# Keeping both halves of one batch's second FFN out of attention, in place of one

## The chip, the cores and the metric

The kernel runs on one core of a Trainium2 chip. The metric is the device time of one execution in microseconds (us). The kernel before has a median of 2063.42 us over 3 runs (2063.11 to 2066.16). All times below are microseconds unless they are marked ns.

A core has five engines that run side by side, each through its own list of instructions in a fixed order: TensorE (PE, matmuls; its weight loads are PEld), VectorE (DVE), ScalarE (ACT), GpSimd (POOL) and SyncE (SP), which here only issues DMA transfers. They wait for one another by semaphores. Matmul results land in PSUM, everything else lives in SBUF.

## The reference

The input is 4 batches of 1024 tokens with 256 features. Each batch goes through three residual blocks:

```
x = x + 0.5 * ffn(layernorm(x))     # first FFN
x = x + attn(layernorm(x))
x = x + 0.5 * ffn(layernorm(x))     # second FFN, the same weights

ffn(x):  scores = sigmoid(x @ gate_W) * route_scale          # 8 experts, the best 2 count
         h = gelu(x @ W1[e] + b1[e]);  y = h @ W2[e] + b2[e]   # for every expert, 256 -> 128 -> 256
         out = sum_e gate[e] * y[e] + shared expert
attn(x): h = softmax(q k / 16 + mask) v @ Wo + bo + x        # 16 heads of 64, 1024 x 1024 scores a head
         out = gelu_tanh(layernorm(h) @ W1 + b1) @ W2 + b2 + h  # an MLP, 256 -> 512 -> 256
```

The reference computes all eight experts for every token and weights them with the gates, and the kernel does the same, so an FFN is dense work: nine experts (the shared one is number 8), each with two small matmuls.

## The kernel before, in words

**Tiling.** Tokens lie on partitions in tiles of 128. An FFN is done for half a batch (512 tokens) at a time, as a *job* (class `Job`, made by `ffn`, line 1086 on): `prep` (layer norm statistics, normalisation L919, turning the tokens so that features lie on partitions, the router), then for each of the nine experts a hidden *layer* (6 matmuls of 512 columns, gelu, times the gate, split into a high and a low 16-bit part), then four *seconds* (one for each tile of 128 tokens, 27 matmuls of 256 columns and one for the bias). Every product is done as three 16-bit matmuls on high and low parts (`mm3`, L970). The attention block's MLP is a job as well (`mlp`), with four layers and four seconds.

**Attention.** A step is one head, half the queries and 256 of the keys. Its loop (`attention`) runs 512 steps. A step's instructions are: maxima of a later step's scores (two matmuls, L1467, and a reduction on DVE, L1474), the scores (four matmuls of 512 columns, L1531 and L1532, into the one PSUM slot S1), the exponential on ScalarE (L570, `pt`), its high part on ScalarE (L1543, `pk`), its low part on GpSimd (L1546), and 24 short matmuls with the values (L1581 to L1584, into `av`). Every fourth step also turns a row of maxima (L1501) and puts it in place (L1505, one DMA).

**Filler.** TensorE's time between these steps is given to other work: projections of later heads (`wq`), output projections of earlier ones (`wo`), and the FFN and MLP jobs (rank 3, generator `serve`). The class `Order` is a planner that runs when the kernel is built: it keeps an estimated clock for every engine, and at each point of the attention loop it picks what TensorE does next by ranks, costs and due times (`pick`, `RATE`, `NEAR`, `LEAD`). What it picks is the order that every engine's list then has; inside attention nothing reorders it.

**Two forms of an FFN.** In attention (`burst` false) the input is turned by DMA (L924, L926, L927), the gates are stored to DRAM (L1068) and come back as eight broadcasts of 256 KB (L1120), and the low part of a hidden piece is made on GpSimd (L1186). In the other form (`burst` true; `spread` in the code) the input is turned by TensorE (L939, evicted at L941 and L943), the gates are spread by a matmul with a selector (L1165), and the low part is made on DVE (L1194).

**The end.** Batch 3 is last. Its own MLPs and second FFNs cannot start before its attention has ended, so they form a tail, done by `run_jobs`: the next job's layers are mixed with the seconds of the one before, and its `prep` is drawn in between. Hidden pieces of neighbouring jobs lie by turns in `hp` and in tiles that attention has left (`pt`, `pk`), inputs by turns in `xF` and `aT`. In this part the order is set by the framework's own scheduler from the program's order.

**KEEP.** The jobs of batch nb-2 = 2 that come after its attention are two MLP halves and two FFN halves, in this order. `queue` puts the last `KEEP` of them on the list `kept`; `serve` does not start a kept job, and `back` gives kept FFN halves the `burst` form. A kept half therefore runs first in the tail. Its `prep` may still be drawn into attention, but `prepare` does so only for the job at the head of the list.

```
            self.kept = jobs[-KEEP:]                                              # queue
        kept = range(2 - KEEP, 2) if b == self.nb - 2 else ()                     # back
                ... and self.jobs[0].prepared and self.jobs[0] not in self.kept   # serve
```

Of the kernel before, what the change touches and what calls it, by code (L numbers as in the profile page):

```python
# [36 lines left out]
CW2 = 32.0  # L37
NOSYNC = mybir.DependencyInfo(mybir.DependencyClass.NoSync, mybir.DependencyReason.DATA)
ORDER = (8, 0, 1, 2, 3, 4, 5, 6, 7)
KEEP = 1  # L40
SPL = 1
OD = 3
TQ = 0
# [264 lines left out]
class Kernel:  # L308
# [1468 lines left out]
    def queue(self, jobs, b=None):  # L1777

        if b == self.nb - 2:
            self.kept = jobs[-KEEP:]  # L1780
        if b == 0:
# [4 lines left out]
    def back(self, b):  # L1786
# [9 lines left out]
        def half_h(half):  # L1796
            return lambda: h[:, half * 4:half * 4 + 4]

        def after(half):
            getattr(nc, QO).dma_start(self.half_of(self.a["out"][b], half), half_h(half)())  # L1800
            yield 0

        m = [self.mlp(b, half, half_h(half)(), burst) for half in range(2)]
        kept = range(2 - KEEP, 2) if b == self.nb - 2 else ()
        self.last = [self.ffn(half_h(half), 2 * b + 1, half, burst or half in kept, lambda half=half: after(half), m[half])
# [122 lines left out]
```

## Time and profile before

| | |
|---|---|
| median of 3 runs | 2063.42 |
| profiled execution, time | 2060.11 |
| its span | 2058.2 |
| mean granted TensorE clock | 0.994 |
| busy: PE / ACT / POOL / DVE | 95% / 73% / 73% / 69% |
| instructions | 53009 |

The profile's page gives each engine's busy time, and the span in 40 slices of 51.5 us with the busy share in tenths. Matmuls overlap in the records: one of 512 columns is shown as 0.38 long, while the next may start 0.215 behind it. So a busy TensorE is not a full one, and the working below counts from start to start. The granted clock is 1.00 or 0.50 in pieces; a stretch's value is their mean. Chains and waits name what ended an idle time last.

Parts of the last 250 us, as they lie in the trace: batch 2's first FFN half has its layers at 1840.5 to 1852.2 in one block, and its seconds spread over the steps up to 1899; the last score step starts at 1912.15; the kept half's layers run from 1926.37 to 1938.45; then come the two MLP halves and the two FFN halves of batch 3, the last matmul at 2053.6.

### The profile page before, as it was taken

To read this page: it belongs to the slowest core of one execution; us is meant where nothing else is said; L and a number is where in the kernel's file an instruction comes from. 1 tells how busy PE (TensorE), PEld (TensorE's weight loads), DVE (VectorE), ACT (ScalarE), POOL (GpSimd) and SP (SyncE) were. 2 spreads that over 40 slices of the span, in tenths; PEclk is the share of its full clock that TensorE was granted. 3 is DMA by queue.
4 is the path that set the end of the run, shared out by engine and by line. 5 is a ranking of instruction groups with operands and counts; after the bars stand their busy time and mean duration, and the time that the engine had idled before them with its cause. 6 is when DMAs were issued, how large, how long until landed. Compare 5 with 4: busy or idle time off the path is not lost. (4 is left out here: it accounts for less than half of the span.)

```text
span 2058.2 us, 53009 instructions
## 1 busy us (share of the span) xinstructions
PE 1960.8 (95%) x22468; PEld 1282.9 (62%) x22468; DVE 1413.6 (69%) x2372; ACT 1499.1 (73%) x1785; POOL 1498.0 (73%) x979
## 2 busy tenths in 40 slices
PE   6989999999999999999999999999999999999878
PEld 2546576766666556666666666656676666667545
DVE  6576676766767777775767667777767576866465
ACT  6437878768766787778787778687877777778563
POOL 7737787768767988778777887777776888778310
PEclk9999999999999999999999999999999999999999
DMA  6543233333513314243333333323324414251000
GB/s 175 152 128 84 75 91 96 75 87 61 143 36 86 89 32 108 49 100 93 81 81 70 98 76 85 92 70 76 81 48 104 114 40 106 48 111 36 11 21 21
DMA packets 213019, 166.21 MB, mean 81 GB/s; under 512 B 140991, under 2 KB 172872, under 8 KB 212782
## 3 DMA queue, kind: packets, MB, share of 16 engines
q1 hardware_dynamic: 212782, 162.83, 32.1%
q8 instruction: 176, 2.88, 0.6%
q14 instruction: 61, 0.50, 0.1%
HBM read 70.18 MB, written 13.83 MB: 41 GB/s over the span
## 5 line engine op out<-in xcount | busy, mean ns | idle before, releaser
L1546 POOL TENSOR_TENSOR pk<-pt,pk 128x1024 f16<-128x1024 f32 x512 | 1087.3, 2132 | 258.9 <-ACT pk L1543 173.0
L1474 DVE TENSOR_REDUCE mx<-S 128x1 f32<-128x1024 f32 x512 | 626.1, 1223 | 298.1 <-PE S L1467 273.1
L570 ACT ACTIVATE pt<-S 128x1024 f32<-128x1024 f32 x512 | 523.8, 1023 | 353.8 <-PE S L1532 334.5
L1543 ACT CAST pk<-pt 128x1024 f16<-128x1024 f32 x512 | 534.6, 1045 | 15.7 <-DMA aT<-pk 0.7
L1584 PE MATMUL av<-V,pk 128*128 128x65 f16 x4096 | 428.7, 192 | 25.7 <-POOL pk L1546 24.7
L1583 PE MATMUL av<-V,pk 128*128 128x64 f16 x4096 | 435.0, 195 | 0.0
L1581 PE MATMUL av<-V,pk 128*128 128x65 f16 x4096 | 434.0, 193 | 0.7 <-DVE at L1597 0.7
L1581 PEld LDWEIGHTS <-pk 128*128 128x128 f16 x4096 | 382.0, 96 | 54.0 <-issue 0.3
L1583 PEld LDWEIGHTS <-pk 128*128 128x128 f16 x4096 | 380.3, 97 | 52.9 <-issue 1.1
L1584 PEld LDWEIGHTS <-pk 128*128 128x128 f16 x4096 | 379.9, 99 | 30.9 <-POOL pk L1546 30.6
L1531 PE MATMUL S<-low 128*128 128x512 f16 x1024 | 388.2, 379 | 6.4 <-ACT pt L570 5.7
L1532 PE MATMUL S<-AC 128*128 128x512 f16 x1024 | 388.4, 379 | 0.0
L1467 PE MATMUL S<-AC 128*128 128x512 f16 x1024 | 304.4, 379 | 7.9 <-DVE mrow L1505 4.7
L970 PEld LDWEIGHTS <-hp 128*128 128x128 f16 x2100 | 204.6, 98 | 71.8 <-issue 6.2
L970 PE MATMUL F<-xA,wq 128*128 128x512 f16 x768 | 187.4, 381 | 0.0
L970 PE MATMUL F<-wfs,hp 128*128 128x256 f16 x1404 | 176.1, 273 | 1.7 <-POOL hp L1186 0.8
L1532 PEld LDWEIGHTS <-AC 128*128 128x128 f16 x1024 | 100.0, 98 | 115.1 <-issue 27.5
L1531 PEld LDWEIGHTS <-low 128*128 128x128 f16 x1024 | 100.0, 98 | 103.9 <-issue 0.6
L1186 POOL TENSOR_TENSOR hp<-u,hp 128x512 f16<-128x512 f32 x88 | 100.5, 1156 | 78.1 <-ACT hp L1183 71.5
L970 PEld LDWEIGHTS <-wfs 128*128 128x128 f16 x864 | 83.7, 99 | 111.3 <-issue 20.9
L970 PE MATMUL F<-xF,wfs 128*128 128x512 f16 x576 | 139.5, 388 | 7.6 <-DVE gb L642 4.2
L970 PEld LDWEIGHTS <-wq 128*128 128x128 f16 x768 | 74.8, 98 | 84.2 <-issue 1.9
(240 smaller groups left out, 2526.2 us busy)
## 6 DMA issues: line engine op xcount, KB each, us to landing
AC<-qk SPq DMA_DIRECT2D x128, 256.0 KB
gb<-gd SPq DMA_DIRECT2D x88, 256.0 KB
low<-qk SPq DMA_DIRECT2D x64, 256.0 KB
wq<-wqd SPq DMA_DIRECT2D x33, 384.0 KB
hp<-mwd SPq DMA_DIRECT2D x6, 1024.0 KB
x<-in_L_attn_x_dram SPq DMA_DIRECT2D x8, 512.0 KB
x1d<-x SPq DMA_DIRECT2D x8, 512.0 KB
wo<-wod SPq DMA_DIRECT2D x16, 256.0 KB
```

The lines of the kernel that those rows point to most:

```text
L570: i = self.nc.scalar.activation(out, in_, func, **kw).ins
L970: i = self.nc.tensor.matmul(*args, start=start, **kw).ins
L1186: nc.gpsimd.tensor_tensor(hp[e][:, 1], u, hp[e][:, 0], ALU.subtract)
L1467: mm(ps[:, hs], AC[:, 0, qs], AC[:, 1, hs], start=True, stop=(h == 0 or t > 0), skip_group_check=True)
L1474: nc.vector.tensor_reduce(self.mx[:, t % 4:t % 4 + 1], ps, AX.X, ALU.max, negate=True)
L1531: mm(o, low[:, 1, ks], low[:, 0, qs], start=True, stop=False, skip_group_check=True)
L1532: mm(o, AC[:, 1, ks], AC[:, 0, qs], start=False, stop=True, skip_group_check=True)
L1543: nc.scalar.copy(pk[:, 0], pt[:])
L1546: nc.gpsimd.tensor_tensor(pk[:, 1], pt[:], pk[:, 0], ALU.subtract)
L1581: mm(o[:, 0:65], pk[:, 0, ps], v[:, 0:65], start=(n == 0 and c == 0 and t == 0), stop=False, skip_group_check=True)
L1583: mm(o[:, 0:64], pk[:, 0, ps], v[:, 65:129], start=False, stop=False, skip_group_check=True)
L1584: mm(o[:, 0:65], pk[:, 1, ps], v[:, 0:65], start=False, stop=(n == 3 and c == 1), skip_group_check=True)
```

## The change

`KEEP` is 2 where it was 1: both halves of batch 2's second FFN are kept, take the `burst` form, and run first behind attention. All other constants, the planner's rate among them, stay.

```
 ORDER = (8, 0, 1, 2, 3, 4, 5, 6, 7)
-KEEP = 1
+KEEP = 2
 SPL = 1
```

With 2, the list's head after the MLP halves is the first FFN half, and it stays there until attention ends; so `prepare` draws the first half's preparation into attention, and the second half's is left to the tail. On TensorE the two kernels' lists agree up to the score step that starts at 1803.89.

## Prediction

> **What bounds the kernel now.** I read the page first.
>
> ```profile
> PE 1960.8 (95%) x22468; PEld 1282.9 (62%) x22468; DVE 1413.6 (69%) x2372; ACT 1499.1 (73%) x1785; POOL 1498.0 (73%) x979
> PE   6989999999999999999999999999999999999878
> POOL 7737787768767988778777887777776888778310
> ```
>
> After the start TensorE is at nine tenths or more until 1904 us and lower behind it, where GpSimd falls to nothing: attention ends there and a tail of FFN work follows. Then the table by stretch, cut at starts of matmuls (columns: stretch, its length, busy PE, PEld, DVE, ACT, POOL, clock, DMA share, GB/s).
>
> ```profile
> 1803.89:1839.67 35.78, 33.96 (x449) 23.19 (x447) 26.58 (x51) 26.78 (x30) 27.88 (x15) 1.00 0.62 127
> 1839.67:1912.15 72.48, 69.53 (x843) 47.08 (x842) 39.78 (x77) 60.39 (x73) 55.71 (x34) 1.00 0.15 42
> 1912.15:1926.37 14.22, 10.26 (x125) 7.41 (x122) 6.34 (x18) 6.44 (x9) 7.13 (x7) 0.88 0.00 1
> 1926.37:1938.45 12.08, 12.08 (x58) 5.47 (x56) 7.15 (x14) 7.18 (x12) 1.60 (x4) 1.00 0.00 0
> 1938.45:1963.93 25.48, 21.02 (x158) 15.14 (x156) 15.29 (x25) 15.11 (x28) 10.12 (x8) 1.00 0.21 62
> 2005.20:2040.38 35.18, 30.38 (x211) 19.20 (x210) 19.99 (x48) 18.39 (x31) 1.60 (x4) 0.95 0.00 1
> ```
>
> In order: stretch A, before the first FFN of batch 2 starts; B, the last 21 score steps, with that FFN between them; C, the end of attention; the hidden layers of the kept FFN alone; its second layers with batch 3's first MLP; and last the "twin", where batch 3's second FFN is laid over its first. TensorE fills A, B and the kept layers; in the twin it does not. Third, what attention does with no FFN between its steps (ScalarE's timeline):
>
> ```profile
> 1819.36 1.02 ACT L570 ACTIVATE pt<-S 128x1024 f32<-128x1024 f32 x1 [0.98 <-PE S L1532]
> 1820.41 1.04 ACT L1543 CAST pk<-pt 128x1024 f16<-128x1024 f32 x1
> 1821.55 1.02 ACT L570 ACTIVATE pt<-S 128x1024 f32<-128x1024 f32 x1
> 1822.61 1.04 ACT L1543 CAST pk<-pt 128x1024 f16<-128x1024 f32 x1
> 1823.75 1.02 ACT L570 ACTIVATE pt<-S 128x1024 f32<-128x1024 f32 x1
> ```
>
> Exponentials start 2.20 apart. One PSUM slot holds the scores: four matmuls (0.86, starts 0.215 apart), their drain, then exp (1.02), then the next four. TensorE needs only 0.73 (values) + 0.43 (maxima) + 0.86 = 2.03 of it. By the starts of L1531, 88 steps of the whole trace hold neither filler nor a row of maxima: median 2.20, mean 2.39. So filler hides 0.17 or more a step, and attention without filler is bound by the score slot and not by TensorE. Last, the chain of waits at the end of attention:
>
> ```profile
> 1919.42 0.20 POOL fnb L901
> ...
> 1919.65 2.07 ACT ld L919 x4
> 1921.73 0.48 ACT aT L1439
> ...
> 1922.22 0.70 DVE aT L1441
> ```
>
> Four normalisations for batch 3's first MLP run on ScalarE ahead of the copy that the last output projection waits for.
>
> **The change part by part.** The instruction order is the same on TensorE until the step at 1803.89. From there batch 2's first FFN leaves B for the tail; its preparation stays in A, in the TensorE form; the second FFN's preparation leaves B for the tail. The sum is against the profiled execution (2060.11, span 2058.2), which lies 3.3 below the median 2063.42; I add the difference to the median.
>
> *A (35.78 now).* Removed: two casts, two GpSimd subtractions (1.16 each) and two transposing DMAs for the input, a gate store, later eight 256 KB broadcasts on SP. SP's other transfers pass earlier; only one DVE wait of 1.9 for a broadcast shows there. Added: two groups of transposes (0.44 each) with their evictions, and four normalisations (2.07) drawn into one ScalarE block. By the new order's steps, each at the length such a step has in the trace: 2.91 (two transposes) + 3.32 + 3.49 + 2.63 (router) + 2.20 + 3.37 + 2.90 + 3.34 + 3.34 + 3.78 + 3.51 = 34.8, so 1.0 less, mostly a 1.53 stall inside the router (waiting for a transposing DMA) that goes. Behind the ScalarE block the exponentials queue, and the values behind them: up to 2.07 back. I take 0.5 less (1.1 more to 1.5 less).
>
> *B (72.48 now).* The 54 first-layer matmuls (0.216 each: 11.7) and 112 second-layer ones (0.109: 12.2) go, with two table loads and the second FFN's transposes, router and gates (1.9). Of the 21 steps, 15 are then bare, 3 carry a row of maxima (17 bare such in the trace, 2.20 to 4.89; the last 2.91), one a row without maxima, one attention's transposes and a selector matmul, one the 12 matmuls of the output projection (3.87 now). 15 x 2.20 + 3 x 2.90 + 2.2 + 2.4 + 3.87 = 50.2. One pair's GpSimd subtraction (L1414, 2.13) was under FFN matmuls; bare, GpSimd (2.09 apart when saturated) regains 0.1 a step, so it delays the values by 0 to 2.13: I take the middle, 1.1. Sum 51.3, saved 21.2. Bounds: rows at 2.20 and no delay 48.0 (saved 24.5); bare steps at the mean and rows at 3.60, 55.4 (saved 17.1). TensorE work of 25.8 leaves, so 4.6 of it does not come back: that is the cover lost.
>
> *C (14.22 now).* The four normalisations for the MLP move behind the kept FFN's hidden layers, so the copy can start at 1919.87 in place of 1921.63: 1.8 less (0 if GpSimd or the table load gates it; 3.1 if the half-clock window in this stretch, clock 0.88, goes with the stall).
>
> *Tail.* One FFN more: layers 11.7, second layers 12.2, eight selector matmuls 1.7, router 0.6, transposes 0.9, gates 0.4: 27.5 of TensorE if all is covered, the lower bound. The first kept FFN's 12.08 of layers stand as they do now; what is inserted is the stretch from their end to the end of the second one's layers. Its order is the twin's: few second-layer matmuls, transposes, router, three layer matmuls, router, fifteen, then the rest mixed. The twin takes 35.18 for the same content; 10.0 of it pass before its router starts, as the first column tile waits for the last hidden piece, and gelu waits for the router's table switch. The four normalisations (2.07) now stand ahead of that switch: upper bound 37.3. Against it the selectors come earlier: after the layers' end DVE has 9 x 0.69 = 6.2 to do for the last pieces, so the router may start some 2 sooner. These about cancel: 35.0. What follows (the MLP's layers, 1938.45 on) keeps its order but for where its layer matmuls lie: 0, give or take 1.
>
> One rule speaks against the change. The Trainium skill, "ScalarE: Activation LUTs", section "What ACT_TABLE_LOAD costs", gives each switch a 1.28 load and a 1.38 drain. In the twin the load at 2015.82 ends at 2017.11 and the router's exp starts at 2017.12: the load agrees, the drain isn't there. The two switches move from attention into the tail's chain; with drains the sum would be 2.8 longer.
>
> Sum: +35.0 - 0.5 - 21.2 - 1.8 = **+11.5**: 2071.6 for a profiled execution, **2074.9** beside the median. Ends: 27.5 - 1.5 - 24.5 - 3.1 = -1.6 and 37.3 + 1.1 - 17.1 + 0 + 1 = +22.3.
>
> **The rivals.** The measurement tells 0.2% (4.1 us) from no change.
> 1. *TensorE is the bound on both sides.* B gives back 24.5, C 1.8, and the second FFN hides its own start: 27.5 - 24.5 - 1.8 - 0.5 = +0.7, 2064. For it: PE 95%. Against it: the twin's 35.18 for 27.5 of work, and 2.20 steps. Chance 0.08.
> 2. *Faster: the extra FFN fills the tail's stalls.* TensorE stands still 4.2 before 1963.93, 1.8 before 1968.45, some 5 between 1976.9 and 1983.6. If the extra second-layer matmuls covered these 11.0 and B gave the full 24.5: 35.0 - 0.5 - 24.5 - 1.8 - 11.0 = -2.8, 2060.6. It decides once over 11.5 are covered at my B, or over 8.2 at that one. Against it: in the new order the extra FFN is done before the MLP's last layer matmuls. Chance 0.03.
> 3. *Attention without filler is slower still.* Bare steps at the mean, rows at 3.60, no gain in C, tail 37.3: 37.3 - 0.5 - 17.1 = +19.7, 2083. For it: several bare steps of 3.2 to 3.9, where GpSimd or ScalarE lag. Chance 0.14.
> 4. *The first FFN is served in attention anyway.* The order shows no layer matmul between the steps of B: 0.
>
> **How the numbers follow.** Forecast 0.75, rivals 0.08, 0.03, 0.14 and 0. Range 2066 to 2083: the lower end is rival 1 with a little lost, the upper rival 3. Slower takes the forecast, rival 3 and a little of rival 1's edge, less the forecast's low edge: 0.88; same 0.08; faster 0.04.
>
> **What would show it.** B's 21 score steps at 50 to 52, exponentials 2.2 apart; eight fewer GpSimd subtractions at L1186, eight fewer broadcasts, eight more selectors at L1165; the copy L1439 with no normalisation ahead of it; 35 between the layers of the two kept FFNs, with TensorE idle before the router. Wrong if steps in B run at 2.05, or if the new stretch in the tail runs at 28 or at 40.

## The result, and the profile after

| | before | changed |
|---|---|---|
| median | 2063.47 (4 runs, 2063.11 to 2066.16) | 2076.57 (4 runs, 2076.37 to 2077.79) |
| profiled execution, span | 2060.11, 2058.2 | 2077.79, 2076.0 |

The changed kernel is slower by 13.1: ratio 1.0067, 95% interval 1.0055 to 1.0079. The forecast was 11.5 slower.

The page of the changed kernel, the lines that answer to those shown of the kernel before:

```profile
PE 1971.0 (95%) x22484; PEld 1287.6 (62%) x22484; DVE 1420.1 (68%) x2382; ACT 1499.4 (72%) x1784; POOL 1487.0 (72%) x969
PE   6989999999999999999999999999999999998888
POOL 7637787768767987778786987877777888776100
```

TensorE's share is still 95%, so the page's first line does not show the change. GpSimd falls to nothing a slice earlier: attention ends earlier and the tail is longer. The table by stretch shows it (changed kernel; columns as in the prediction: stretch, length, busy PE, PEld, DVE, ACT, POOL, clock, DMA share, GB/s):

```profile
1806.50:1843.10 36.60, 34.79 (x456) 24.23 (x455) 28.27 (x55) 27.83 (x33) 27.95 (x17) 1.00 0.41 95
1843.10:1894.65 51.55, 46.51 (x642) 29.41 (x641) 24.59 (x32) 44.45 (x44) 45.21 (x22) 1.00 0.08 17
1894.65:1905.91 11.26, 8.39 (x123) 6.62 (x120) 5.17 (x16) 4.26 (x5) 6.24 (x7) 1.00 0.01 2
1905.91:1918.00 12.09, 12.09 (x59) 5.48 (x56) 7.49 (x17) 7.19 (x12) 1.60 (x4) 1.00 0.01 1
1918.00:1953.02 35.02, 30.98 (x216) 20.16 (x215) 19.88 (x46) 17.78 (x30) 3.23 (x3) 0.95 0.09 27
1953.02:1979.87 26.85, 20.46 (x154) 14.78 (x153) 15.72 (x26) 16.20 (x29) 6.87 (x6) 0.98 0.13 44
2022.58:2057.97 35.39, 30.55 (x212) 19.48 (x210) 19.82 (x48) 18.38 (x31) 1.60 (x4) 0.95 0.00 1
```

In order: A, B, C, the layers of the first kept FFN, the inserted stretch to the end of the second kept FFN's layers, the stretch to the end of the first MLP's layers, and the twin. B lost 21 and its TensorE is busy for 46.5 of 51.6; the inserted stretch has the twin's length and its idle time. Set beside the kernel before, with a second execution of the same changed kernel (first experiment) to tell run from change, all between starts or ends of the same matmuls:

| part | before | changed | changed again | forecast of the difference |
|---|---|---|---|---|
| up to the first changed step | 1803.89 | 1806.50 | 1805.45 | 0 |
| A | 35.78 | 36.60 | 36.61 | -0.5 |
| B | 72.48 | 51.55 | 51.58 | -21.2 |
| C | 14.22 | 11.26 | 12.16 | -1.8 |
| layers of the first kept FFN | 12.08 | 12.09 | 12.09 | 0 |
| inserted FFN | - | 35.02 | 34.62 | +35.0 |
| to the end of the first MLP's layers | 25.48 | 26.85 | 26.72 | 0, give or take 1 |
| second MLP's layers | 12.99 | 13.81 | 12.75 | 0 |
| batch 3's first FFN | 28.28 | 28.90 | 28.61 | 0 |
| twin | 35.18 | 35.39 | 35.51 | 0 |
| rest | 17.8 | 18.0 | 18.0 | 0 |

The first row is no effect of the change. In the 14 traces of this study the first score step starts at 154.5 to 158.2 and the way from there to the first changed step takes 1648.5 to 1652.3, for all kernels alike; before's trace has the smallest sum of the two. So the spans differ by 17.8 and the medians by 13.1. From the first changed step on the parts add up to +15.2 and, for the repeat, +14.3; the 1 to 2 by which this is above the medians is within what single traces of one kernel differ by here.

ScalarE's timeline in B, where nothing is left between the score steps:

```profile
1854.20 1.02 ACT L570 ACTIVATE pt<-S 128x1024 f32<-128x1024 f32 x1 [1.22 <-PE S L1532]
1855.26 1.04 ACT L1543 CAST pk<-pt 128x1024 f16<-128x1024 f32 x1
1856.40 1.02 ACT L570 ACTIVATE pt<-S 128x1024 f32<-128x1024 f32 x1
1857.45 1.05 ACT L1543 CAST pk<-pt 128x1024 f16<-128x1024 f32 x1
1858.60 1.02 ACT L570 ACTIVATE pt<-S 128x1024 f32<-128x1024 f32 x1
1859.65 1.04 ACT L1543 CAST pk<-pt 128x1024 f16<-128x1024 f32 x1
1860.87 1.02 ACT L570 ACTIVATE pt<-S 128x1024 f32<-128x1024 f32 x1 [0.17 <-PE S L1532]
```

Exponentials start 2.20 apart, as forecast, and once 2.27. Of B's 21 steps fourteen take 2.19 to 2.27 and one 2.48; three with a row of maxima take 3.32, 3.28 and 3.24; one in which GpSimd also subtracts for attention's output takes 3.17; one with transposes 2.25; the one with the output projection 2.90. The chain of waits across C:

```profile
1901.77 0.67 PE F L1436 x4
1902.46 0.59 ACT aT L1439
1903.08 0.70 DVE aT L1441
1903.83 10.02 PE F L970 x55
```

The copy L1439 follows the transposes at once; no normalisation stands ahead of it. And ScalarE in the inserted FFN:

```profile
1925.55 0.58 ACT L941 CAST aT<-S 128x512 f16<-128x512 f32 x1 [1.33 <-PE S L939]
1926.03 1.09 ACT L919 ACTIVATE ld<-h,fnb,fr 128x256 f32<-128x256 f32 x2
1927.64 0.58 ACT L941 CAST aT<-S 128x512 f16<-128x512 f32 x1 [0.53 <-PE S L939]
1928.13 1.09 ACT L919 ACTIVATE ld<-h,fnb,fr 128x256 f32<-128x256 f32 x2
1929.24 1.28 ACT L570 ACT_TABLE_LOAD   x1
1930.53 0.18 ACT L570 ACTIVATE S<-S 128x32 f32<-128x32 f32 x1
1930.73 1.28 ACT L570 ACT_TABLE_LOAD   x1
1932.03 0.66 ACT L570 ACTIVATE F<-F,b1f 128x512 f32<-128x512 f32 x1
```

The first kept FFN's layers ended at 1918.00; the second one's first gelu runs at 1932.03, behind its transposes' evictions, two pairs of the MLP's normalisations, and the router's exp between two table loads. Exp starts 0.01 and gelu 0.02 behind its load: no drain.

### The profile page after: what moved, and what is told of

Its sections match the earlier page's. It is cut to its first block, busy times and chain, and to the rows that moved or that the text cites. A ratio compares the mean times of both kernels' runs of the same rounds, so it can differ in the third digit from the quotient of the medians.

```text
span 2076.0 us, 53017 instructions
## 1 busy us (share of the span) xinstructions
PE 1971.0 (95%) x22484; PEld 1287.6 (62%) x22484; DVE 1420.1 (68%) x2382; ACT 1499.4 (72%) x1784; POOL 1487.0 (72%) x969
## 3 DMA queue, kind: packets, MB, share of 16 engines
HBM read 68.09 MB, written 13.81 MB: 39 GB/s over the span
## 4 chain that ended last, share of the span: by engine, by line
PE 81%; POOL 6%; ACT 5%; DVE 4%; issue 2%; DMA 1%; SPq 0%; POOLq 0%; ACTq 0%; DVEq 0%
PE F L970 32%; PE S L1531 10%; PE S L1467 10%; PE S L1532 9%; PE av L1584 6%; PE av L1583 5%; PE av L1581 5%; POOL pk L1546 3%; PE S L970 2%; ACT pt L570 1%; ACT pk L1543 1%; DMA gb<-gd 1%; POOL hp L1186 1%; PE S L1501 1%; ACT u L570 1%
## 5 line engine op out<-in xcount | busy, mean ns | idle before, releaser
L970 PEld LDWEIGHTS <-hp 128*128 128x128 f16 x1992 | 195.5, 99 | 85.2 <-issue 11.2
L970 PE MATMUL F<-wfs,hp 128*128 128x256 f16 x1296 | 166.0, 274 | 7.8 <-ACT hp L1183 3.8
L1186 POOL TENSOR_TENSOR hp<-u,hp 128x512 f16<-128x512 f32 x80 | 91.5, 1158 | 72.3 <-ACT hp L1183 68.7
L970 PE MATMUL F<-xF,wfs 128*128 128x512 f16 x540 | 132.0, 391 | 7.7 <-DVE gb L642 4.2
```

The lines of the kernel that those rows point to most:

```text
L970: i = self.nc.tensor.matmul(*args, start=start, **kw).ins
L1186: nc.gpsimd.tensor_tensor(hp[e][:, 1], u, hp[e][:, 0], ALU.subtract)
```

## The experiments

Medians of one group of runs stand beside the kernel before of the same group (2062.82 in the first, 2063.52, 2063.93 and 2061.89 in the others).

**1. The changed kernel again.**

> The changed kernel once more, to see which stretches of the two traces differ from run to run and which by the change. Theory (the change acts only from the step at 1803.89 of before on): the stretch ahead of it, 2.61 longer in the changed kernel's trace, comes out anywhere between 1803.9 and 1806.5; B stays at 51 to 52, C at 11 to 11.5, the inserted FFN at 35.0, each within 0.3 of the first trace. The two MLP stretches (26.85 and 42.71) move by up to 1.4 if their surplus over before is run-to-run, and stay within 0.3 if it belongs to the new order. Rival: the stretch ahead is again 2.6 longer, so something of the change lies in the early part too.

2076.19 (5 runs), ratio 1.0068 (1.0056 to 1.0080). A, B, the inserted FFN and the twin repeat within 0.4. The stretch ahead came out 1.05 shorter than the first time. Of the two MLP stretches the first keeps its surplus over before (26.72 against 25.48), so that belongs to the new order; the second does not (12.75 against 12.99). C does not repeat either: 12.16 at a clock of 0.86 against 11.26 at 1.00.

**2. What attention gives back when a job leaves it and none is added.** Batch 2's first second-FFN half is left out altogether:

```
-        return m + self.last
+        if b == self.nb - 2:
+            m[0].after = lambda: after(0)
+            return m + self.last[1:]
+        return m + self.last
```

> The kernel before, one half kept, with batch 2's first second-FFN half left out altogether: that half of batch 2 is written without its second FFN. This is what attention gives back when a job leaves it, with no job added behind. Theory of the prediction (attention without filler is bound by its score slot, 2.20 a step): B falls by 20 to 22, A and C within 1 of before or C shorter by up to 3, time 2039.5 to 2043.5, against TensorE work of 27.5 that was left out. Rival (TensorE is the bound, a job costs what its matmuls cost): 25.8 to 29.5 less, 2034 to 2037.6.

2042.53 (4 runs), ratio 0.9904 (0.9891 to 0.9916): 20.3 less, inside the theory's range and outside the rival's. Its A and B:

```profile
1807.83:1841.63 33.80, 31.84 (x429) 21.30 (x427) 25.09 (x43) 26.62 (x30) 27.12 (x17) 1.00 0.40 95
1841.63:1895.41 53.78, 48.91 (x671) 31.86 (x670) 29.45 (x51) 45.51 (x46) 46.16 (x22) 1.00 0.09 21
```

A and B together lose 20.7, split otherwise than expected (A 2.0 less, B 18.7). The 27.5 in the expectation are those of the other form of an FFN; the half that was left out turns its input by DMA and has no selectors, so 11.7 + 12.2 + 0.6 + 0.4 = 24.9 of TensorE work left the kernel by the prediction's prices, and the time fell by 20.3: 4.6 of the work did not come back as time. With this run the whole change falls into two measured halves: -20.3 for taking the job out, and 2076.19 - 2042.53 = +33.7 for putting it into the tail.

**3. Is a bare step bound by the score slot or by TensorE?** The changed kernel, with a third of the value products of the last 21 steps left out:

```
-                mm(o[:, 0:65], pk[:, 1, ps], v[:, 0:65], start=False, ...)
+                if i < 491 or n == 3 and c == 1:
+                    mm(o[:, 0:65], pk[:, 1, ps], v[:, 0:65], start=False, ...)
```

> The changed kernel, where the products of the values with the low part of the probabilities are left out in the last 21 steps (8 of 24 value matmuls a step, 0.24 of TensorE's time); GpSimd still makes the low part. Theory of the prediction (a step without filler is bound by the score slot: scores, their drain, exp): bare steps stay at 2.20, B falls by 0 to 2 (only steps with rows or projections get shorter), time 2074 to 2077. Rival (TensorE bounds the bare steps): they fall to 1.96, B falls by 4 to 5, time 2071 to 2072.

```profile
1842.52:1893.33 50.81, 42.96 (x519) 25.57 (x518) 24.36 (x32) 44.23 (x44) 44.89 (x22) 1.00 0.11 17
```

B takes 50.81, 0.7 less, with 3.6 less of busy PE than in the changed kernel (46.51). Fifteen steps stand at 2.19 or 2.20. TensorE's work does not bound them. The time (2078.67 from 4 runs, 2075.37 to 2080.45) is above the range that the theory gave; the profiled span is 2073.6, so the runs of this kernel scatter by more than the 0.7.

Two rivals remain for a bare step of 2.20: ScalarE, busy for 1.02 + 1.04 of it, and GpSimd, busy for 2.13. The records speak against both. In the changed kernel's trace 79 exponentials start less than 2.3 behind the one before with nothing but the cast between them; all 79 start 0.10 behind the recorded end of the last score matmul. Behind the end of the cast they start by 0.09 to 0.18, while an activation that waits for nothing starts 0.09 to 0.10 before the recorded end of a cast (L919 at 1926.03 above, behind the cast of 1925.55). So ScalarE would be ready about 0.19 sooner: it waits for the scores. GpSimd's subtractions start 2.20 apart in bare steps, but 2.09 apart where they are queued (1867.28, 1869.36, 1871.45). And in this run most values no longer read GpSimd's part: the step that took 3.17 takes 2.20, and the next row's step, whose last values still read it, takes 4.14 in place of 3.24. What is left is the loop through the one score slot.

**4. Why the inserted FFN takes 35.0.** The changed kernel, with the second kept half's preparation also drawn into attention. It needs a tile that attention has left free; and the MLP's normalisations are held behind the first kept FFN's hidden layers, where they already were:

```
+            job = following()      # the first of the two jobs at the head that is not yet prepared
...
-            xt = self.half_tile(half if spread and slot == 0 else None)
+            xt = self.half_tile(half if spread and (slot == 0 or slot == 2 * self.nb - 3 and half) else None)
...
+                if self.last_hi and not self.order:
+                    self.tc.add_manual_dep(n, self.last_hi, NOSYNC, reason="behind the hidden layers")
```

> The changed kernel, with the second kept half's preparation (transposes, router, gates) also drawn into attention's last steps, its turned input in a tile that attention has left free, and the four normalisations for batch 3's first MLP held behind the first kept FFN's hidden layers, as they already lie in the changed kernel. The work is the same. Theory of the prediction (the inserted FFN costs 35.0 and not 27.5 because 10 of it pass before its router starts and gelu waits for a table switch behind it): the stretch between the ends of the two kept FFNs' layers falls to 25.6 (27.5 of TensorE work less 1.5 for transposes and router) to 28, B takes 1.5 to 3 more for those transposes and the router; in all 5 to 8 less than the changed kernel, 2069 to 2071. Rival (hidden pieces and PSUM hold the stretch back, not the preparation): the stretch stays at 33 to 35, B takes 1.5 to 3 more, time 2077 to 2079.

2065.18 (11 runs), ratio 1.0011 (1.0003 to 1.0020): 11.0 less than the changed kernel, more than expected. Its B and its stretch between the ends of the two kept FFNs' layers:

```profile
1842.51:1895.47 52.96, 47.98 (x679) 31.17 (x678) 32.09 (x63) 47.71 (x53) 46.60 (x26) 1.00 0.08 18
...
1918.82:1944.45 25.63, 25.56 (x174) 16.84 (x172) 14.49 (x23) 16.25 (x30) 5.07 (x4) 1.00 0.07 22
```

The stretch falls from 35.02 to 25.63, TensorE full and at clock 1.00; B takes 1.4 more; the MLP's stretch falls by 2.5 (24.36). The second layers, hidden pieces and selectors are the same as before, so 9.4 of the 35.0 were the preparation and what waits for it.

**5. Part C alone.** The kernel before, with the four normalisations for batch 3's first MLP held behind the kept FFN's hidden layers (and the MLP's preparation not drawn between those layers):

```
-                prep_next()
+                if pending:
+                    prep_next()
...
+                if self.last_hi and not self.order:
+                    self.tc.add_manual_dep(n, self.last_hi, NOSYNC, reason="behind the hidden layers")
```

> The kernel before, with only the four normalisations for batch 3's first MLP held behind the kept FFN's hidden layers. This is the change's part C by itself; the work is the same. Theory (these 2.07 on ScalarE stand ahead of the copy that the last output projection waits for, and the half-clock window comes from that stall): C falls from 14.22 to 11.0 to 12.4, the rest stays, time 1.8 to 3.1 below before: 2060.4 to 2061.7. Rival (the wait moves on: the MLP's transposes then wait for the normalisations): C falls by as much, the stretch behind the kept layers (25.48) grows by 1 to 3, time within 1 of 2063.4.

2063.72 (12 runs), ratio 1.0002 (0.9992 to 1.0012): nothing. The stretches C, first and second MLP:

```profile
1916.74:1928.06 11.32, 8.72 (x125) 6.71 (x121) 5.89 (x17) 4.48 (x5) 7.13 (x7) 1.00 0.01 1
1940.15:1966.50 26.35, 21.92 (x157) 15.51 (x156) 15.31 (x25) 15.95 (x30) 9.29 (x8) 0.94 0.19 60
1966.50:1980.52 14.02, 11.39 (x73) 6.68 (x71) 8.70 (x20) 7.82 (x14) 2.21 (x5) 0.99 0.01 2
```

The rival holds in the total: C loses 2.9, the first MLP's stretch gains 0.9 (the rival said 1 to 3) and the second's 1.0. The normalisations now run from 1948.32, the MLP's transposes wait for them, and its first layer matmul starts 12.70 behind the kept layers (1952.84) where it started 12.10 behind them (1950.55). That is 0.6 of the 1.9; the rest, in part at clock 0.94, is not explained. C also shows what part of its loss is the clock. At clock 1.00 it takes 12.84, 12.85 and 12.91 where the normalisations lie in it (ScalarE has 9 instructions there; experiments 2, 7 and 6), and 11.26, 11.26 and 11.32 where they don't (5 instructions; changed kernel, experiments 4 and 5). So they cost 1.6. The rest of before's 14.22 is a half-clock window (0.88), which the repeat of the changed kernel shows without them (12.16 at 0.86).

**6. The twin, entered sooner.** The kernel before, where the second MLP's seconds are mixed twice as densely into the first FFN's layers, and the second FFN's preparation begins when they are through:

```
-                due += pending[0].cost / job.pieces if pending else 0.0
+                due += (2 if pending[0].pieces < job.pieces else 1) * pending[0].cost / job.pieces if pending else 0.0
...
+                        if pending and last is None and not pending[0].done:
+                            last = pending[0]
+                            yield from end()
+                        for _ in range(3):
+                            prep_next()
```

> The kernel before, where the second MLP half's seconds are mixed twice as densely into the layers of batch 3's first FFN, and the job counts as done when they are through, so that the second FFN's preparation can start some four layers sooner. The work is the same. Theory (the twin takes 35.2 for 25.6 to 27.5 of TensorE work because its preparation begins when the layers ahead are over): the twin falls to 29 to 32, time 2057 to 2060.5. Rival (DVE's hidden pieces of the first FFN stand ahead of the preparation's pieces wherever it begins): the twin stays within 1 of 35.2, time 2062.5 to 2064.

2063.84 (11 runs), ratio 1.0003 (0.9995 to 1.0012). The twin stays at 35.56. Its transposes and its router still lie behind the first FFN's layers, among that FFN's seconds. The transposes start sooner, 2.85 behind the layers' end (2009.66) in place of 6.99, but the router starts later, 12.43 behind it in place of 10.04, with twelve of the twin's own layer matmuls ahead of it. Drawing a preparation earlier a piece at a time does not get its gates there before the layers.

**7 and 8. Another order of the tail's jobs.** Call the kept halves k0 and k1, the MLP halves m0 and m1, batch 3's FFNs f0 and f1. Run 7 is the changed kernel in the order k0 m0 m1 k1 f0 f1, run 8 the kernel before in the order m0 m1 k0 f0 f1:

```
                 self.pipe = True
+                k0, k1, m0, m1, f0, f1 = self.jobs          # run 7
+                self.jobs = [k0, m0, m1, k1, f0, f1]
+                k0, m0, m1, f0, f1 = self.jobs              # run 8
+                self.jobs = [m0, m1, k0, f0, f1]
```

> The changed kernel, with the tail's six jobs in another order: first kept FFN half, both MLP halves of batch 3, then the second kept FFN half, then batch 3's two FFN halves. The work is the same. Theory (an extra FFN costs 35 in the tail because its input's preparation and the waits of its neighbours lie open; TensorE work of an FFN is 27.5): between the MLPs and batch 3's FFNs its layers run beside the second MLP's seconds, and the preparations of batch 3's FFNs, whose inputs are then done one job earlier, run beside it. The layers of the first kept FFN 12.1 and the MLPs 26.5 and 13.5 as in the changed kernel, the second kept FFN 17 to 20, batch 3's FFNs 25.6 to 29 each: 120 to 129 from the end of attention to the last layers in place of 151, time 2045 to 2054, below the kernel before. Rival (the end is bound by hidden pieces on DVE and ScalarE, not by preparations): each FFN still takes 33 to 35 from layers to layers, 2070 to 2076.

> The kernel before, one half kept as before, but the kept FFN put behind batch 3's two MLP halves in place of ahead of them, and the second MLP's input in a tile that attention has left free. The work is the same. It tells the order from the number of halves that are kept. Theory of open preparations: with nothing between the last output projection and the first MLP some 8 of its preparation lie open; in return the FFNs of batch 3 take 25.6 to 29 each in place of 28.3 and 35.2. From the end of attention to the last layers 98 to 106 in place of 114, time 2047 to 2056. Rival (the MLP chain bounds the tail whatever lies between): 112 to 118, 2061 to 2067.

Run 7: 2077.88 (5 runs), ratio 1.0072 (1.0059 to 1.0086). Run 8: 2067.73 (8 runs), ratio 1.0022 (1.0012 to 1.0033). Neither theory nor rival holds. In run 7 k1 takes 24.8, f0 40.9 and f1 27.1; in run 8 k0 20.3, f0 41.2 and f1 27.1. The last FFN has become cheap and the one before it dear. In run 7 f0's router starts at 1995.5, behind k1's layers (which end at 1989.5), though its input, the first MLP's output, was done by 1960: it is drawn one piece at a time between those layers, and f0's hidden pieces wait for its gates.

**9 and 10. Gates ahead of layers.** The orders of runs 8 and 7, with the next FFN's preparation put ahead of the layers of the job before it as soon as its input is done; run 10 also has experiment 4's preparations in attention:

```
+            if self.jobs and self.jobs[0].dep and self.jobs[0].dep.done:
+                for _ in self.jobs[0].prep:
+                    pass
```

> The kernel with one half kept behind the two MLP halves, and the preparation of a following FFN (normalisation, transposes, router, gates) put in the program ahead of the layers of the job before it, as soon as its input is done, in place of a piece at a time between those layers. The work is the same. Theory (an FFN takes 25.6 to 28 where its gates are there before its layers, and 33 to 41 where they come behind them, because all its hidden pieces then wait): from the last score step on 26.8 to the end of the first MLP's layers and 19.3 for the second as in the kernel with one half between; the kept FFN's layers 21 to 25 in place of 20.3, since the router now lies ahead of them; batch 3's FFNs 27 to 31 in place of 41.2, and 26 to 28; in all 120 to 131 in place of 134.7, time 2053 to 2064. Rival (DVE's work, some 20 for an FFN's pieces and router, is the bound, wherever the gates are): the 41.2 falls to 35 to 38 and the others rise by as much, time 2066 to 2070.

> The changed kernel with both kept halves' preparations in attention and late normalisations (as in the run of that name), and with the second kept half behind batch 3's MLP halves, each following FFN's preparation ahead of the layers of the job before it. The work is the same. Theory (gates ahead of layers make an FFN cost its TensorE time): 12.1 for the first kept FFN's layers, 24.4 to 27 and 12.7 to 14 for the MLPs, 19 to 25 for the second kept FFN beside the second MLP's seconds, 27 to 31 and 26 to 28 for batch 3's FFNs: 121 to 137 in place of the 138.7 of the run with both preparations in attention, time 2049 to 2063.5. Rival (DVE and ScalarE bound the tail, and what is gained in one job is given back in the next): 137 to 142, 2064 to 2068.

Run 9: 2061.88 (11 runs), ratio 0.9990 (0.9981 to 0.9999), within the theory's range and the one version below the kernel before, by about what a measurement can tell. Run 10: 2067.02 (11 runs), ratio 1.0018 (1.0009 to 1.0027), in the rival's range. The kept FFN, f0 and f1 of run 9:

```profile
1955.68:1981.92 26.24, 22.25 (x143) 12.73 (x144) 19.16 (x51) 16.66 (x30) 0.00 (x0) 0.87 0.00 1
1981.92:2016.24 34.32, 30.02 (x213) 19.63 (x212) 19.48 (x48) 18.14 (x31) 1.61 (x4) 0.95 0.00 1
2016.24:2041.47 25.23, 25.22 (x169) 16.35 (x168) 14.69 (x24) 11.89 (x20) 0.00 (x0) 1.00 0.06 21
```

f1, whose gates are there, takes 25.23 (run 10: 25.24). f0 takes 34.3 in both, since f1's router now lies in it: TensorE stops for 2.85 ahead of the matmul at 1996.44 in run 9, while ScalarE does the router's exp and loads gelu's table; gelu is back at 1995.12.

**11 and 12. Both routers ahead of all gelu work.** As 9 and 10, with the second MLP's seconds done first and both preparations behind them:

```
+            if pending and len(self.jobs) == 2 and self.jobs[1].dep is pending[0]:
+                for c in other:
+                    yield c
+                last = pending[0]
+                yield from end()
+                for _ in self.jobs[1].prep:
+                    pass
```

> The kernel with one half kept behind the two MLP halves, where in addition the second MLP's seconds are done before the kept FFN's layers and both of batch 3's FFN preparations follow them, so that both routers lie ahead of all gelu work and no table switch is left between the last three FFNs. The work is the same. Theory (a router between an FFN's hidden pieces stops TensorE, since gelu waits for the table switch and a PSUM bank comes free only by gelu): batch 3's first FFN takes 25.2 to 27 in place of 34.3, its second 25.2 to 26.5, the kept FFN 28 to 33 in place of 26.2 as both preparations now lie open ahead of it; from the last score step to the last layers 118 to 127 in place of 125.8, time 2053 to 2062. Rival (DVE and ScalarE take 33 or more for a pair of FFN and preparation wherever the router lies): 127 to 132, 2063 to 2068.

> The same with two halves kept (both prepared in attention, the first ahead of the MLP halves, the second behind them). The work is the same. Theory: 12.1 for the first kept FFN's layers, 25.8 and 13.3 for the MLPs as in the run with both in attention and one between, 28 to 33 for the second kept FFN with both preparations of batch 3, 25.2 to 27 and 25.2 to 26.5 for batch 3's FFNs: 130 to 138 in place of 137.7, time 2059 to 2067; about what the one with one half kept takes plus 3 to 6, since attention does not give back 4 to 5 of the second half's TensorE time. Rival (an FFN costs the same in the tail as in attention once its gates are there): within 1 of the one with one half kept.

Run 11: 2066.81 (9 runs), ratio 1.0024 (1.0014 to 1.0034). Run 12: 2073.11 (5 runs), ratio 1.0054 (1.0041 to 1.0067). The kept FFN, f0 and f1 of run 11:

```profile
1953.28:1994.25 40.97, 29.30 (x177) 15.95 (x178) 24.55 (x75) 20.72 (x38) 1.61 (x4) 0.79 0.00 1
1994.25:2020.33 26.08, 25.88 (x171) 16.45 (x170) 15.55 (x25) 12.61 (x21) 0.00 (x0) 1.00 0.01 1
2020.33:2046.37 26.04, 26.04 (x178) 17.33 (x177) 13.33 (x23) 11.42 (x19) 0.00 (x0) 1.00 0.06 21
```

The theory is right on the FFNs and wrong on the time: both take 26, TensorE full, and the stretch ahead of them takes 41 with TensorE at a clock of 0.79. The two preparations now lie open there. The stretches side by side, from the end of one job's layers to the end of its own:

| run | m0 | m1 | kept FFN | f0 | f1 | sum |
|---|---|---|---|---|---|---|
| changed kernel (k1 ahead of m0) | 26.85 | 13.81 | 35.02 | 28.90 | 35.39 | 139.97 |
| 4, both prepared in attention (k1 ahead of m0) | 24.36 | 12.74 | 25.63 | 28.39 | 35.44 | 126.56 |
| 7 | 27.17 | 16.15 | 24.82 | 40.87 | 27.12 | 136.13 |
| 10 | 25.77 | 13.30 | 27.01 | 34.27 | 25.24 | 125.59 |
| 12 | 25.80 | 13.30 | 41.41 | 26.08 | 26.04 | 132.63 |

An FFN stretch with the gates there costs 25.2 to 26.1, in seven places (runs 4 and 9 to 12). A preparation that lies in the tail costs 7 to 11 wherever it is put: 9.4 in the changed kernel, 34.32 - 25.23 = 9.1 in f0 of run 9, and 7.6 in its kept FFN (26.24 less 11.7 of layers, 5.2 of the MLP's seconds and 1.7 of selectors), 22.4 for the two in run 11 (40.97 less the same). The orders mostly moved it about; only attention hides it, for 1.4. With two halves kept the same scheme takes 5.1 (9 and 10) and 6.3 (11 and 12) more than with one: between the cover that attention loses, 4.6, and that with the 2.6 which the second form has more of TensorE work, 7.2. What stays open is why two preparations in a row cost more (22.4) than two apart (16.7). The clock differs too (0.79 over run 11's 40.97; 0.87 and 0.95 in run 9), and how much of these costs is the clock no run separates.

## Why the prediction was right

The mechanism and the sign are as forecast; the sum was 11.5 and the medians give 13.1 and 13.4. By its steps:

- **B, -21.2.** Measured -20.9 in both traces. Two sizes in it cancelled: steps with a row of maxima were taken at 2.90 and took 3.24 to 3.32; the one with the output projection was taken at 3.87 and took 2.90. The GpSimd subtraction was taken at 1.1 and took 0.97. The other steps add 0.2. The row steps are longer for a reason that lies on DVE. First the row of the kernel before that gave the 2.91, then one of the changed kernel:

```profile
1824.77 0.28 DVE L1505 TENSOR_SCALAR mrow<-S 4x128 f16<-4x128 f32 x1
1824.98 0.16 DVE L1596 RECIPROCAL rc<-av 128x4 f32<-128x4 f32 x1
```

```profile
1861.70 0.18 DVE L1596 RECIPROCAL rc<-av 128x4 f32<-128x4 f32 x1 [0.54 <-PE av L1584]
1861.92 0.42 DVE L1597 TENSOR_TENSOR at<-av,rc 128x256 f32<-128x256 f32 x1
1862.26 0.27 DVE L1505 TENSOR_SCALAR mrow<-S 4x128 f16<-4x128 f32 x1
```

The row's L1505 frees the slot for the next maxima. In the changed kernel's three row steps the norm of a finished group of values (L1596, L1597) stands ahead of it, and TensorE waits 0.81 to 0.88 for it; in the step that set the price L1505 came first, and TensorE waited 0.37.

- **The cover lost, 4.6.** In the changed kernel it is 25.8 - 20.9 = 4.9. That TensorE work of a job does not all come back is shown by experiment 2 as well (4.6 of 24.9; that the number is the same is chance, as 2.0 of the 20.3 came from A there). That TensorE is not the bound of a bare step is shown by experiment 3, and that the score slot is, by the records given there.
- **The tail, +35.0.** 35.02 and 34.62. That the twin's order gives the twin's length was the right choice among the bounds, and experiment 4 shows the reason that the prediction gave: with the preparation gone the stretch takes 25.63, where the lower bound less 1.5 for transposes and router is 26.0. The two corrections that were set against each other (the normalisations 2.07 later, the router some 2 sooner) did not show at their sizes: the router's matmuls start 9.66 behind the layers' end and 10.04 in the twin, the first gelu 14.03 and 14.27. That they cancel was right, their sizes were not shown.
- **A, -0.5.** The sign was wrong: +0.8, in both traces. The steps were each taken at the length of a like step; seven of eleven came out within 0.06, four took 1.76 more. The last took 4.48 for 3.51, and the one at 1824.63, where the norm stands ahead of the row as in B, 3.25 for 2.90. In the last the row's transposition waits behind the output projection's matmuls, and the next maxima wait 0.81 for the row (L1505). The 1.9 of DVE's wait for a broadcast that was read in A lies in B (1854.25); A holds one of 1.02 (1838.07). A's 0.8 lies inside the bounds (1.1 more).
- **C, -1.8.** The normalisations cost 1.6 (experiment 5). The trace's -2.96 has a half-clock window on top that before's trace had in C and the changed one's hadn't. That window is not the stall's, as the upper bound of 3.1 supposed: the repeat had it without the stall.
- **What follows, 0 give or take 1.** This is the term that was mis-sized: +1.2 to +1.4 in the first MLP's stretch and 0.3 to 0.6 in batch 3's first FFN. The wait of experiment 5 is not the one here: the four normalisations are done at 1929.22, 15 ahead of the MLP's first transposes (1944.59). The MLP's first layer matmul (1967.76) starts 14.74 behind the layers ahead of it, 2.64 later than before's. On the way TensorE stands still four times, for 2.7 in all, for hidden pieces of the second kept FFN (0.32 for ScalarE's cast, 0.19 and 1.12 for gelu, 1.05 for DVE's low part), with the second MLP's normalisations between the pieces on ScalarE (from 1953.63), and the second MLP's transposes also come ahead of that matmul. Behind it 1.3 comes back. No run takes this apart, so the cause of the 1.2 to 1.4 stays open. C and this term together are near zero, where the sum had -1.8.

Rival 1 (TensorE bound) asked for an inserted stretch of 27.5 and a B 24.5 shorter, and got neither; rival 2 (faster, the extra FFN fills stalls) asked that 11.5 be covered, and the MLP's stalls stayed. Experiment 4 shows that the mechanism of rival 2 exists, by way of the preparation and not of the stalls named: 11.0 were to be had, which still left the kernel 2.4 behind the one before. Eight fewer subtractions (L1186: 88 to 80), eight fewer broadcasts (L1120: 88 to 80) and eight more selectors (L1165: 24 to 32) came as forecast.

The rule on table loads that was weighed (the Trainium skill, "ScalarE: Activation LUTs", "What ACT_TABLE_LOAD costs") had the load right at 1.28 and its drain is again not in the trace: exp at 1930.53 behind a load from 1929.24, gelu at 1932.03 behind one from 1930.73. With two drains at the page's figure the inserted FFN is estimated at 37.8, and it took 35.0.

## What to carry to other kernels

A job that is moved out of a pipelined loop pays twice: the loop gives back less than the job's matmuls (20.3 of 24.9 here, since what it stood beside has a limit of its own), and in its new place its preparation lies open (9.4 here) unless that is moved apart from it and left behind in the loop. Price such a move by the nearest stretch with the same order of instructions, not by its engine time: the twin gave 35.2 for the 35.0 measured, TensorE's content 27.5. And where a short stall goes from one stage, look for the same instructions in the next one before it is counted as a gain.

## What was not expected of the hardware

The half-clock windows of TensorE do not have a fixed place in the program. Behind the same idle of 3.71 the same 24 matmuls of the changed kernel took 5.07 to the next start in one execution and 4.29 in the other (2.6 at full clock); the first two lines are of the changed kernel's timeline of TensorE, the other two of its repeat's:

```profile
1979.87 5.28 PE L970 MATMUL F<-qk,hp 128*128 128x256 f16 x24 [3.71 <-ACT u L570]
1984.94 1.73 PE L970 MATMUL F<-aT,qk 128*128 128x512 f16 x6
```

```profile
1979.22 4.45 PE L970 MATMUL F<-qk,hp 128*128 128x256 f16 x24 [3.71 <-ACT u L570]
1983.51 1.46 PE L970 MATMUL F<-aT,qk 128*128 128x512 f16 x6
```

In C the window came in one of the two executions and not in the other (clock 0.86 and 1.00, 0.9 apart). The Trainium skill, "TensorE: Matmul & The Clock Gate", section "Part 1: The HAM clock gate (the "warmup" mystery)", says that the gate watches a free-running window, so that the place of the change varies from run to run; these rows agree, though no run here shows the gate's window itself. A stretch's clock in a single trace is therefore no property of the stretch, and a difference of one to two in a stalled stage wants a second trace.
